# Layer 1's context prepared inside layer 0, first keys resized on VectorE, and a new order of one slot: a four-layer network on one Trainium2 core

## The chip, the cores and the metric

The kernel runs on one core of a Trainium2 chip, as one launch. The time is the device time of that core in microseconds (us). It was run three times: 6812.18 us is the median, 6793.82 and 6815.5 us are the ends. The core has TensorE (PE), VectorE (DVE), ScalarE (ACT), GpSimd (POOL) and SyncE (SP). Each takes its instructions in order; semaphores join them. SP here only issues DMAs.

## What is computed

An image `x` of shape (2, 128, 64, 64), all in float32, goes through four layers one after the other. Only what the change touches is written out:

```
layer 0:  x_norm = layernorm over channels, 4096 tokens per image
          for four orders (rows forward, rows reversed, columns forward, columns reversed):
              xh, z = x @ W_in ; xh = silu(causal conv of 4 taps (xh))
              dt, B, C = split(xh @ W_xp) ; dt = softplus(dt @ W_dt + b)
              h[t] = exp(dt*A) * h[t-1] + dt*B*xh        (256 channels x 16 states)
              y = sum over states of C*h + D*xh ; y = y * silu(z) ; y @ W_out
          x = x + fuse(the four outputs)
layer 1:  ctx = bilinear resize of context (4 images in, 2 used, each a mix over the batch axis;
                                            256 channels, 32x32 to 64x64)
          q = Wq x + bq ; k = Wk ctx + bk ; v = Wv ctx + bv
          x = x + gamma * conv3x3(softmax(q.k) v)
layer 2:  x = x + Wo softmax-attention(x) + bo
layer 3:  a second, smaller state-space layer on 16-channel groups, group norm, silu
```

The resize commutes with the 1x1 convolutions. So the kernel mixes the context images (weights 3/7, 3/7, 1/7), projects them to keys and values at 32x32, stores these four small images in DRAM (`low`), and resizes pieces of them when attention needs them.

## The kernel before

**Layer 0** works on 64 chunks of 512 tokens: 2 images x 2 orders x 2 directions x 8 chunks. I number them 0 to 63. A chunk has 16 units `u`, each a 128x1024 piece of the state. The loop `for k, c in enumerate(chunks)` holds a loop over 16 slots `s`, and the order of every engine's queue is the order in which this loop issues (`tc.manual_schedule()`). In slot `s` of chunk `c` it issues, in this order:

- POOL: `s_dbu(s+2)` (L330), the product that feeds a scan two slots later; three buffers `dbu`
- DVE: `s_scan(s)` (L374), the recurrence; then an optional step `V[s]`
- DVE or POOL: `s_hc(s-1)` (L386 on DVE, L384 on POOL for units 0, 5, 9, 11, 14), state times C
- ACT: `s_da(s+1)` (L343, two instructions, into one of two PSUM buffers), `s_fix(s+1)` (L355 and L358: the carry between chunks is added into `dbu`), `s_hst` (L379), then the steps `A[s]`
- PE: `y0` and the sums over states `s_y` (L390, L397), then the step `M[s]`, then `s_pc` (L363), which spreads C for a later `s_hc`

The steps `A`, `M`, `V` prepare the next chunks. The chunk after this one is `new`, the one after that `nxt`. For `nxt`: `px(0)` in `M[8]` and `px(1)` in `M[10]` (L228, the 4-tap convolution as four matmuls each), their results read by `x_(0)` in `A[9]` and `x_(1)` in `A[12]` (L237), `xsilu` in `A[13]`, and `pd` in `M[15]` (L267). For `new`: `xd_` in `A[0]` (L272, reads the result of `pd`, and issues two DMAs of `rows`), `pt(0)` in `M[0]` (L287, needs `xd_`), `abs_`, `e_exp`, `e_ln` in `A[1]` to `A[3]` (L294 to L300; `e_ln` costs two loads of an activation table). All of `px`, `pd`, `pt`, `pz`, `po` and the norm's matmuls share one PSUM bank, `misc`: each waits until the reader of the one before is done. The gate `yg_` (L404, DVE) reads the finished sums: `yg_(0)` in slot 10, `yg_(1)` in slot 1 of the next chunk.

Twelve chunks do a part of the layernorm as well: chunks 0 to 4 (`norms[0..3]` and its second halves) and 15 to 23. I call chunks 1 to 4 and 16 to 23 norm chunks, and the other chunks normal.

**Opening** of layer 0 (before chunk 0): both images of `x` are loaded (L74), the first four norm blocks are done, the first chunk's quantities are made.

**Between the layers**: when layer 0's buffers are free, SP loads `m3`, `cw3`, `dtw3`, `m1`, `m2` and four context images (L662 to L726); PE and DVE combine two weights of layer 2 (`wvo`, `bo`, L705 to L710); DVE mixes (L731 to L733); PE projects into four banks (L740), ACT copies with bias (L742) and pads by one row at each end (L744, L745); SP stores `low` (L746). Then `resize` makes the first two key pieces in five steps: load a piece `lo` (L799), `wide` on ACT (L804 to L807), `wide2` on POOL (L813), `high` on ACT (L818, L819), `high2` on POOL (L824). Then the first query, and then the attention of layer 1.

**Layers 1 and 2** run as one pipeline of 64 groups of 256 queries, 16 slots each; the later pieces of keys and values are put into slots by `piece` and `put`. **Layer 3** is not touched but for where `m3`, `cw3` and `dtw3` are loaded.

Of the kernel before, what the change touches and what calls it, by code (L numbers as in the profile page):

```python
# [56 lines left out]
def conv_seq_kernel(ctx: ExitStack, tc: tile.TileContext, a: dict, out: bass.AP):  # L57
# [12 lines left out]
    xin = a["x"].rearrange("b c h w -> c b (h w)")  # L70
    for b in range(B):
        for lo, hi in ((0, 1), (1, 2), (2, 4), (4, 8)):
            sl = slice(lo * T, hi * T)
            nc.sync.dma_start(x[:, b, sl], xin[:, b, sl])  # L74
    nc.scalar.dma_start(vec, a["vec"])
    nc.scalar.dma_start(cst, a["cst"])

    def v(name):
        return vec[:, _V[name] : _V[name] + 1]
# [8 lines left out]
    act(aneg, vec[:, _VA0:_NV], AF.Exp)  # L88
    nc.vector.tensor_scalar(aneg, aneg, -1.0, None, ALU.mult)

    with ExitStack() as c0:
# [21 lines left out]
        nc.scalar.dma_start(m0, a["m0"][:, 0 : 256 + 2 * ND])  # L116
        nc.scalar.dma_start(w_dt[64:ND, :], a["wdt"])
        w_xT, w_out, w_fT = mt[:, 0:256], mt[:, 256:512], mt[:, 512:1024]
        w_zT = m0[:, 0:256]
# [20 lines left out]
        for t in (xn, xnt):  # L140
            nc.vector.memset(t[:, 0:3], 0.0)
            nc.vector.memset(t[:, L + 3 : L + 6], 0.0)

        def gq(u):
# [298 lines left out]
        with tc.manual_schedule():  # L443
# [64 lines left out]
            for i in range(2):  # L508
                nc.vector.tensor_scalar(diag_d[:, i, :], ident, v(f"dp{i}"), None, ALU.mult)
            for j in (2, 3):  # L510
                act(sqs[j], xcs[j], AF.Square)
# [19 lines left out]
            act(r[:, 8:16], vr[:, 8:16], AF.Sqrt, bias=eps)  # L531
            nc.vector.reciprocal(r[:, 8:16], r[:, 8:16])
            for i in range(2):
                c1.px(i, ba[i])
# [21 lines left out]
            for k, c in enumerate(chunks):  # L556
# [15 lines left out]
                if new is not None:  # L572
                    A[0] = (new.xd_,)
                    M[0], A[1] = lambda: new.pt(0), (lambda: new.abs_(0),)
                    M[1], A[2] = lambda: new.pt(1), (lambda: new.abs_(1), new.e_exp)
                    A[3] = (new.e_ln,)
                    M[4], V[5] = lambda: new.pt(0), lambda: new.dt_(0)
                    M[5], V[6] = lambda: new.pt(1), lambda: new.dt_(1)
                    G[7], G[8] = lambda: new.dtu_(0), lambda: new.dtu_(1)
                    if not new.rev:  # L580
                        M[6], A[7] = lambda: new.pz(0), (lambda: new.z_(0),)
                        M[13], A[14] = lambda: new.pz(1), (lambda: new.z_(1),)
                if nxt is not None:
                    M[8], A[9] = lambda: nxt.px(0), (lambda: nxt.x_(0),)
                    M[10], A[12] = lambda: nxt.px(1), (lambda: nxt.x_(1),)
                    A[13] = (nxt.xsilu,)
                    M[15] = nxt.pd
                if lp is not None:
                    A[3] = (*A[3], lp.ln, lp.exp)
                    A[6] = (lp.rows,)  # L590
                    M[7], V[8] = lp.scale, lp.mul
                    A[10] = (lp.affine,)
                if ln is not None:
                    M[12], V[13] = ln.center, ln.sub
                    A[14] = (*A.get(14, ()), ln.square)
                    M[14], A[15] = ln.var, (ln.keep,)
                if k in turns:
                    A[11] = (lambda: turn(turns[k]),)

                for s in range(16):  # L600
# [9 lines left out]
                    if s in G:  # L610
                        G[s]()

                    if c1 is not None:
                        c1.s_da(u1)
                        c1.s_fix(u1)
# [4 lines left out]

                    if s in (3, 11):
                        c.y0(s // 11)
                    for cy, e in ((c, s), (old, s + 16)):
                        for u in pairs.get(e, ()) if cy is not None else ():
                            cy.s_y(u)
                            cy.s_y(u + 1)
                    if s in M:
# [33 lines left out]
    dtw3 = gt([P, 32], "dtw3", late)  # L661
    nc.sync.dma_start(m3, a["m3"])  # L662
    nc.sync.dma_start(cw3, a["cw3"].partition_broadcast(P))
    nc.sync.dma_start(dtw3, a["dtw3"].partition_broadcast(P))

# [3 lines left out]
    with ExitStack() as c1:  # L669
# [7 lines left out]
        ps = c1.enter_context(tc.tile_pool(name="ps1", bufs=1, space=PSUM))  # L677
        dr = c1.enter_context(tc.tile_pool(name="dr1", bufs=1, space=bass.MemoryType.DRAM))

        m1 = gt([P, 1792], "m1", wp)  # L680
        m2 = gt([P, 512], "m2", wp)
        nc.sync.dma_start(m1, a["m1"])
        nc.sync.dma_start(m2, a["m2"])
        w1qT = m1[:, 0:128]
        w1kT = m1[:, 128:384].rearrange("p (k c) -> p k c", k=2)
        w1vT = m1[:, 384:640].rearrange("p (k c) -> p k c", k=2)
        w1pT = m1[:, 640:1792].rearrange("p (k c) -> p k c", k=9)
# [11 lines left out]
        def small(tag, shape, bufs=None):  # L699
# [3 lines left out]
        wvo = gt([P, P], "wvo", wp)  # L703
        pw = misc()
        mm(pw[:, :P], lhsT=w2v, rhs=w2oT, start=True, stop=True)  # L705
        nc.vector.tensor_copy(wvo, pw[:, :P])
        bo = gt([P, 1], "bo", wp)
        pw = misc()
        mm(pw[:, :1], lhsT=w2oT, rhs=v("bv2"), start=True, stop=True)
        nc.vector.tensor_add(bo, v("bo2"), pw[:, :1])  # L710

# [4 lines left out]
        nc.gpsimd.memset(pad, 0.0)  # L716


        low = [[dr.tile([P, 34, 32], F32, tag=f"low{b}{w}", name=f"low{b}{w}") for w in range(2)]
               for b in range(B)]  # L720
        cfeat = a["ctx"].rearrange("b (k p) h w -> p b k (h w)", p=P)
        with ExitStack() as cc:
            cx = cc.enter_context(tc.tile_pool(name="ctx", bufs=1))
            feat = [cx.tile([P, 2, 1024], F32, tag=f"ct{j}", name=f"ct{j}") for j in range(4)]
            for j in range(4):
                nc.sync.dma_start(feat[j], cfeat[:, j])  # L726
            for b in range(B):

                wts = (3 / 7, 3 / 7, 1 / 7) if b == 0 else (1 / 7, 3 / 7, 3 / 7)
                mix = cx.tile([P, 2, 1024], F32, tag="mix", name="mix", bufs=2)  # L730
                nc.vector.tensor_scalar(mix, feat[b], wts[0], None, ALU.mult)  # L731
                nc.vector.scalar_tensor_tensor(mix, feat[b + 1], wts[1], mix, ALU.mult, ALU.add)
                nc.vector.scalar_tensor_tensor(mix, feat[b + 2], wts[2], mix, ALU.mult, ALU.add)  # L733

                for w, (wT, bias) in enumerate(((w1kT, v("bk1")), (w1vT, v("bv1")))):
                    t = cx.tile([P, 34, 32], F32, tag="lo", name="lo", bufs=2)
                    for hf in range(2):
                        pl = bank("s", bufs=4)
                        for k in range(2):
                            mm(pl, lhsT=wT[:, k, :], rhs=mix[:, k, hf * T : (hf + 1) * T],  # L740
                               start=(k == 0), stop=(k == 1))
                        act(t[:, 1 + 16 * hf : 17 + 16 * hf, :], pl.rearrange("p (h w) -> p h w", w=32),  # L742
                            AF.Identity, bias=bias)
                    nc.scalar.copy(t[:, 0:1, :], t[:, 1:2, :])  # L744
                    nc.scalar.copy(t[:, 33:34, :], t[:, 32:33, :])  # L745
                    nc.sync.dma_start(low[b][w], t)  # L746

        sp_ = c1.enter_context(tc.tile_pool(name="s", bufs=13))

        class Job:  # L750
# [42 lines left out]
            def resize(self, w, qd, dst):  # L793

                st = {}

                def load():
# [11 lines left out]
                def wide2():  # L809
                    hz = st["hz"] = small("hz", (P, 10, W), bufs=1)  # L810
                    o = hz.rearrange("p h (w two) -> p h w two", two=2)
                    for e in range(2):
                        nc.gpsimd.tensor_add(o[:, :, :, e], st["lo"], st["q"][:, :, 2 * e : 2 * e + 32])  # L813

# [6 lines left out]
                def high2():  # L821
                    o = dst.rearrange("p (h two w) -> p h two w", two=2, w=W)
                    for e in range(2):
                        nc.gpsimd.tensor_add(o[:, :, e, :], st["t"], st["hz"][:, 2 * e : 2 * e + 8, :])  # L824

# [101 lines left out]
        class Conv:  # L927
# [13 lines left out]
            def end(self):  # L941
# [3 lines left out]
                nc.gpsimd.tensor_add(xo, xo, t)  # L945

        jobs = [Job(1, 0), Job(1, 1), Job(2, 0), Job(2, 1)]
        groups = [Group(j, g) for j in jobs for g in range(NG)]
# [34 lines left out]
        with tc.manual_schedule():  # L983
            for qd in range(2):
                for f in jobs[0].key_piece(qd):
                    f()
            piece(1, jobs[0], "key_piece", 2)
            piece(5, jobs[0], "key_piece", 3)
            for qd in range(4):
                piece(10 + 5 * qd, jobs[0], "value_piece", qd)  # L990
            groups[0].q = jobs[0].query(0)

# [555 lines left out]
```

## Time and profile before

| what | value |
|---|---|
| three runs | 6793.82, 6812.18 (median), 6815.5 us |
| the profiled execution's own time | 6810.44 us |
| its span in the profile | 6808.7 us |
| busy: PE, DVE, ACT, POOL | 6005.6, 5524.3, 4461.8, 5362.4 us |
| granted TensorE clock, mean | 0.857 |

The span is 1.7 us shorter than the execution's own time, and that time is 1.7 us below the median. In the profile the first scan starts at 57.2 us, layer 0's last matmul ends at 3480.5 us, the first score of layer 1 starts at 3523.7 us, and layer 3 starts near 5690 us. A row of the timeline gives the start, the duration and in brackets the idle time before it with what ended that; rows of one kind that follow each other are merged (x2, x8).

### The profile page before, as it was taken

The numbers are of one execution on the slowest core, as the hardware profiler recorded it, in microseconds if no ns is written. First come the engines' busy times: TensorE is split into PE (matmuls) and PEld (weight loads), VectorE is DVE, ScalarE is ACT, GpSimd is POOL, SyncE is SP. The second block draws the span as 40 slices with busy tenths as digits, with TensorE's granted clock in tenths as the row PEclk, the third lists the DMA queues.
The fourth block names the chain that finished last, engine by engine and source line by source line (L and its number), as shares of the span: only waits on it lengthen the run. The fifth ranks groups of instructions, "written<-read, shape, count | busy, mean of one in ns | idle before, by whom it ended". The sixth has DMA issues, their size and how long they took to land. (4 is left out here: it accounts for less than half of the span.)

```text
span 6808.7 us, 67303 instructions
## 1 busy us (share of the span) xinstructions
PE 6005.6 (88%) x20652; PEld 2821.7 (41%) x20652; DVE 5524.3 (81%) x4499; ACT 4461.8 (66%) x7666; POOL 5362.4 (79%) x2487
## 2 busy tenths in 40 slices
PE   8888888888888888888879999999999997888888
PEld 2222222222222222222238887787788884222222
DVE  7999999999999999999966665565566675787777
ACT  7887778877788777887745664555456564434342
POOL 6899998899999999999956664555566666777776
PEclk7777777777778777777779999999999998988888
DMA  6565655566566656665630000000000001222221
GB/s 170 138 149 145 157 145 140 137 154 150 141 159 152 157 143 154 150 154 146 148 93 2 4 4 1 1 1 1 1 1 13 1 1 61 75 71 72 90 75 67
DMA packets 352652, 616.51 MB, mean 91 GB/s; under 512 B 72473, under 2 KB 74786, under 8 KB 351650
## 3 DMA queue, kind: packets, MB, share of 16 engines
q1 hardware_dynamic: 351552, 610.44, 35.2%
q8 instruction: 162, 2.65, 0.2%
q14 instruction: 200, 1.64, 0.1%
q10 hardware_dynamic: 738, 1.78, 0.1%
HBM read 496.45 MB, written 115.47 MB: 90 GB/s over the span
## 5 line engine op out<-in xcount | busy, mean ns | idle before, releaser
L330 POOL TENSOR_TENSOR dbu<-dus,bs 128x1024 f32<-128x1024 f32 x1024 | 2404.0, 2374 | 157.0 <-DVE h L374 141.1
L374 DVE TENSOR_TENSOR_SCAN h<-da,hst,dbu 128x1024 f32<-128x1024 f32 x896 | 2094.3, 2345 | 77.8 <-ACT dbu L358 75.0
L343 ACT ACTIVATE da<-dts,aneg 128x512 f32<-128x512 f32 (+1 forms) x2048 | 1412.6, 690 | 443.7 <-DVE h L374 404.1
L890 POOL TENSOR_TENSOR sum<-sum,sc 128x1024 f32<-128x1024 f32 x384 | 906.8, 2362 | 496.7 <-ACT sc L885 493.1
L852 ACT COPY sc<-s 128x512 f32<-128x512 f32 x1024 | 598.1, 585 | 867.7 <-PE s L847 753.5
L859 DVE TENSOR_TENSOR mx<-mx,s 128x512 f32<-128x512 f32 x896 | 610.1, 681 | 569.5 <-ACT sc L852 568.5
L847 PE MATMUL s<-q,k 128*128 128x256 f32 x4096 | 1058.0, 382 | 11.7 <-ACT q L833 8.4
L902 PE MATMUL av<-sc,v 128*128 128x256 f32 x4096 | 1049.6, 379 | 2.3 <-ACT sc L885 2.3
L397 PE MATMUL y<-hc,cst 128*32 128x512 f32 x4096 | 811.3, 760 | 179.2 <-DVE hc L386 103.8
L386 DVE TENSOR_TENSOR hc<-h,pc 128x1024 f32<-128x1024 f32 x704 | 844.9, 1200 | 0.1
L847 PEld LDWEIGHTS s<-q,k 128*128 128x128 f32 x4096 | 781.2, 192 | 146.2 <-issue 36.6
L902 PEld LDWEIGHTS av<-sc,v 128*128 128x128 f32 x4096 | 769.1, 190 | 103.1 <-ACT sc L885 3.7
L384 POOL TENSOR_TENSOR hc<-h,cs 128x1024 f32<-128x1024 f32 x320 | 758.2, 2369 | 1.3 <-issue 1.3
L363 PE MATMUL pc<-xd,sel 16*128 16x512 f32 x1024 | 713.4, 788 | 4.8 <-DVE hc L386 4.1
L1217 POOL TENSOR_TENSOR A<-A,D 128x1024 f32<-128x1024 f32 x224 | 525.9, 2365 | 225.2 <-DVE D L1222 200.3
L882 DVE TENSOR_TENSOR sc<-sc,pm 128x1024 f32<-128x1024 f32 x512 | 620.9, 1214 | 0.9 <-PE pm L878 0.9
L885 ACT ACTIVATE sc<-sc 128x1024 f32<-128x1024 f32 x512 | 542.3, 1059 | 8.6 <-DVE sc L882 8.1
L287 PE MATMUL misc<-xd,w_dt 9*128 9x512 f32 x504 | 386.5, 855 | 155.1 <-ACT x L426 83.6
L1210 ACT ACTIVATE A<-dtr,aneg 128x1024 f32<-128x1024 f32 (+1 forms) x256 | 246.0, 1032 | 380.8 <-PE y L1242 363.0
L397 PEld LDWEIGHTS y<-hc,cst 128*32 128x32 f32 x4096 | 104.9, 117 | 745.6 <-issue 337.4
L1228 DVE TENSOR_TENSOR A<-A,q 128x1024 f32<-128x1024 f32 (+1 forms) x256 | 276.9, 1082 | 148.4 <-PE q L1194 148.2
L1194 PE MATMUL q<-xs,lb 32*128 32x512 f32 x896 | 331.5, 712 | 72.0 <-DVE D L1204 65.7
(263 smaller groups left out, 8078.4 us busy)
## 6 DMA issues: line engine op xcount, KB each, us to landing
dts<-ddt SPq DMA_DIRECT2D x512, 256.0 KB, 5.5
dus<-ddu SPq DMA_DIRECT2D x512, 256.0 KB, 5.1
bs<-rows SPq DMA_DIRECT2D x1024, 64.0 KB, 4.9
cs<-rows SPq DMA_DIRECT2D x1024, 64.0 KB, 3.3
ddt<-dt SPq DMA_DIRECT2D x128, 256.0 KB, 2.0
ddu<-dtu SPq DMA_DIRECT2D x128, 256.0 KB, 4.1
dtr<-ddt SPq DMA_DIRECT2D x448, 64.0 KB, 1.9
rx<-ddx SPq DMA_DIRECT2D x448, 64.0 KB, 1.9
```

The costliest lines, as they stand in the source:

```text
L330: nc.gpsimd.tensor_mul(t, self.dus[q], _bc(self.bs[g], 1, [P, 2, T]))
L343: act(t[:, i, sl], self.dts[q][:, i, sl], AF.Exp, scale=an[:, g, 2 * q + i : 2 * q + i + 1])
L363: mm(t, lhsT=sel[32:48, 4 * g : 4 * g + 4, :].rearrange("p n d -> p (n d)"), rhs=self.xd[32:48, :], start=True, stop=True)
L374: nc.vector.tensor_tensor_scan(ho, ai, bi, init, ALU.mult, ALU.add)
L384: nc.gpsimd.tensor_mul(t, self.h[u], _bc(self.cs[gq(u)[0]], 1, [P, 2, T]))
L386: nc.vector.tensor_mul(t, self.h[u], _bc(self.pc[u // 2], 1, [P, 2, T]))
L397: mm(self.y[q // 2][r : r + 32, :], lhsT=sum4, rhs=self.hc[u][:, i, :], start=False, stop=(u % 8 >= 6), skip_group_check=True)
L847: mm(p[:, o, :], lhsT=j.k[m // 8][:, m % 8 * P : m % 8 * P + P], rhs=self.q, start=True, stop=True)
L859: nc.vector.tensor_max(self.mx, self.s[0][:, 0:2, :] if u == 1 else self.mx, self.p[u])
L882: nc.vector.tensor_sub(s, s, _bc(self.pm[:, :], 1, [P, 4, NQ]))
L890: nc.gpsimd.tensor_add(self.sum, self.s[0] if w == 1 else self.sum, self.s[w])
L902: mm(self.av, lhsT=self.job.v[m // 8][:, m % 8, :], rhs=self.s[u // 2][:, m % 4, :], start=(m == 0), stop=(m == 31))
```

## The change

It has four parts.

1. **The context.** Image 1 of `x` is no longer loaded in the opening; it is loaded in chunks 9 to 12, one quarter each. The four context images are loaded by SP in the opening instead, into the free halves of `xnt`, two `h` and two `dbu` buffers. VectorE mixes them in place: `mixed(0)` behind the two `diag_d` instructions, `mixed(1)` behind the second reciprocal. In chunks 0 to 7 a step `Low.conv` (two matmuls into `misc`) is `M[8]` and `Low.out` (one ACT instruction into a free part of `x`, two DMAs to `low`) is in `A[9]`.
2. **The order of layer 0.** In all chunks `px(0)` moves from `M[8]` to `M[9]`, `x_(0)` from `A[9]` to `A[10]` (behind `affine` in norm chunks). `xd_` moves from the end of slot 0's ACT work to its front, ahead of `s_da(1)`, `s_fix(1)` and `s_hst`. The sums `y0` and `s_y` are issued ahead of ACT's part; on PE's own queue nothing changes by that, since only ACT instructions stood between.
3. **Between the layers.** Loads, mixing, projection, copies and stores of `low` are gone from there. The first piece of keys is loaded first, then the 128 columns of `m1` that the query needs, the second piece, and the rest of `m1` and `m2`. The first query stands between the first and the second key piece. The third and fourth key pieces are put one slot earlier (0 and 4 in place of 1 and 5). `wvo` and `bo` are made in slot 6, the loads for layer 3 are issued in slot 7.
4. **The resize.** `wide2` and `high2` of the four key pieces of image 0 run on VectorE in place of GpSimd.

```diff
-    for b in range(B):
-        for lo, hi in ((0, 1), (1, 2), (2, 4), (4, 8)):
-            nc.sync.dma_start(x[:, b, sl], xin[:, b, sl])
+    for lo, hi in ((0, 1), (1, 2), (2, 4), (4, 8)):
+        nc.sync.dma_start(x[:, 0, sl], xin[:, 0, sl])
...
+        w_kv = x[:, 1, 0:512].rearrange("p (w k c) -> p w k c", w=2, k=2)
+        nc.scalar.dma_start(x[:, 1, 0:512], a["m1"][:, 128:640])
...
+        for k in range(2):
+            nc.sync.dma_start(mix[0][k], cfeat[:, 0, k])
+        for j in (1, 2):
+            for k in range(2):
+                feat[j, k] = wt("h" if j == 1 else "dbu", NH if j == 1 else NDBU, (P, 1024))
+                nc.sync.dma_start(feat[j, k], cfeat[:, j, k])
+        for k in range(2):
+            nc.sync.dma_start(mix[1][k], cfeat[:, 3, k])
+        def mixed(b):
+            w = (3 / 7, 3 / 7, 1 / 7) if b == 0 else (1 / 7, 3 / 7, 3 / 7)
+            for k in range(2):
+                m = mix[b][k]
+                nc.vector.tensor_scalar(m, m, w[0 if b == 0 else 2], None, ALU.mult)
+                for j in (1, 2):
+                    nc.vector.scalar_tensor_tensor(m, feat[j, k], w[j - b], m, ALU.mult, ALU.add)
+        class Low:
+            def conv(self):
+                self.p = misc()
+                for k in range(2):
+                    mm(self.p, lhsT=w_kv[:, self.w, k, :], rhs=mix[self.b][k][:, self.hf * T : self.hf * T + T],
+                       start=(k == 0), stop=(k == 1))
+            def out(self):
+                t = x[:, 1, T * (1 + self.hf) : T * (2 + self.hf)]
+                act(t, self.p, AF.Identity, bias=v("bv1" if self.w else "bk1"))
+                nc.sync.dma_start(o[:, 32 + T * self.hf : 32 + T * self.hf + T], t)
+                ... # and one row of padding
...
                 if new is not None:
-                    A[0] = (new.xd_,)
...
-                    M[8], A[9] = lambda: nxt.px(0), (lambda: nxt.x_(0),)
+                    M[9], A[10] = lambda: nxt.px(0), (lambda: nxt.x_(0),)
...
-                    A[10] = (lp.affine,)
+                    A[10] = (lp.affine, *A.get(10, ()))
...
+                if k < 8:
+                    lw = Low(k // 4, k % 4 // 2, k % 2)
+                    M[8], A[9] = lw.conv, (*A.get(9, ()), lw.out)
+                if 9 <= k < 13:
+                    sl = slice(2 * T * (k - 9), 2 * T * (k - 8))
+                    nc.sync.dma_start(x[:, 1, sl], xin[:, 1, sl])
...
+                    if s in (3, 11):
+                        c.y0(s // 11)
+                    for cy, e in ((c, s), (old, s + 16)):
+                        for u in pairs.get(e, ()) if cy is not None else ():
+                            cy.s_y(u)
+                            cy.s_y(u + 1)
+                    if s == 0 and new is not None:
+                        new.xd_()
                     if c1 is not None:
                         c1.s_da(u1)
                         c1.s_fix(u1)
...
-                    if s in (3, 11):
-                        c.y0(s // 11)
-                    for cy, e in ((c, s), (old, s + 16)):
-                        ...
+                eng = nc.vector if self.b == 0 and w == 0 else nc.gpsimd
-                        nc.gpsimd.tensor_add(o[:, :, :, e], st["lo"], st["q"][:, :, 2 * e : 2 * e + 32])
+                        eng.tensor_add(o[:, :, :, e], st["lo"], st["q"][:, :, 2 * e : 2 * e + 32])
...
-            for qd in range(2):
-                for f in jobs[0].key_piece(qd):
-                    f()
-            piece(1, jobs[0], "key_piece", 2)
-            piece(5, jobs[0], "key_piece", 3)
+            k0, k1 = (jobs[0].key_piece(qd) for qd in range(2))
+            k0[0]()
+            nc.sync.dma_start(m1[:, 0:128], a["m1"][:, 0:128])
+            k1[0]()
+            nc.sync.dma_start(m1[:, 128:], a["m1"][:, 128:])
+            nc.sync.dma_start(m2, a["m2"])
+            for f in k0[1:]:
+                f()
+            groups[0].q = jobs[0].query(0)
+            for f in k1[1:]:
+                f()
+            piece(0, jobs[0], "key_piece", 2)
+            piece(4, jobs[0], "key_piece", 3)
...
-            groups[0].q = jobs[0].query(0)
+            put(6, second, thirds)
```

## The prediction, made before the changed kernel was run

> **What bounds the kernel now.** I read the 40 slices of the page first. They divide the span into layer 0 (VectorE and GpSimd nearly full), a dip, and layers 1 and 2 (TensorE full).
>
> ```profile
> PEclk7777777777778777777779999999999998988888
> DVE  7999999999999999999966665565566675787777
> POOL 6899998899999999999956664555566666777776
> ```
>
> Then the windows by class of chunk. After the colon stand the length and each engine's busy time.
>
> ```profile
> core 0: us, PE busy (x) PEld busy (x) DVE busy (x) ACT busy (x) POOL busy (x), PEclk, DMA share, GB/s
> 914.00:1371.00 457.00, 388.61 (x1068) 114.76 (x1066) 417.59 (x265) 378.44 (x732) 411.59 (x186) 0.77 0.57 140
> 1371.00:3478.00 2107.00, 1787.91 (x4750) 482.93 (x4749) 2037.54 (x1241) 1676.28 (x3176) 2041.11 (x917) 0.77 0.61 149
> 3478.00:3524.00 46.00, 21.25 (x44) 9.26 (x43) 12.05 (x9) 12.84 (x30) 10.07 (x8) 0.76 0.49 183
> ```
>
> The 40 last chunks take 2107/40 = 52.7 us with VectorE and GpSimd busy for 97% each: a new order can win back at most 1.7 us of VectorE's idle time in each. The eight norm chunks of the first row take 57.1 us, of which VectorE idles (457 - 417.6)/8 = 4.9 us. The last row is the passage from layer 0 to layer 1: 46 us in which no engine is busy for half the time. It holds the sure gain, so I read its timeline; then the waits of VectorE in layer 0, and one normal and one norm chunk.
>
> ```profile
> DVE h L374 <- ACT dbu L358: 75.0, 129, 1.4
> DVE dt L404 <- PE y L397: 38.8, 36, 2.4
> ```
>
> **The passage.** In before the chain is: layer 0's last matmul ends 3480.5, context loads, VectorE's mixing from 3491.2, projection, store of `low`, load of a piece, resize, query, first score.
>
> ```profile
> 3491.22 1.23 DVE L731 TENSOR_SCALAR mix<-ct 128x2048 f32<-128x2048 f32 x1 [0.99 <-DMA ct<-in_ctx_dram]
> 3499.68 16.60 PE L740 MATMUL s<-mix,m 128*128 128x512 f32 x32 [9.64 <-DVE mix L733]
> 3509.72 0.34 SPq L799 DMA_DIRECT2D lo<-low  x1
> 3512.01 0.47 ACT L804 ACTIVATE q<-lo 128x320 f32<-128x320 f32 x1
> 3514.43 1.59 POOL L813 TENSOR_TENSOR hz<-lo,q 128x320 f32<-128x320 f32 x2 [30.10 <-ACT lo L807]
> 3517.59 2.49 POOL L824 TENSOR_TENSOR k<-h,hz 128x512 f32<-128x512 f32 x2 [1.57 <-ACT hz L819]
> ```
>
> After: the load of `lo` goes out at 3480.6 and lands 2.3 later (here 3509.72 to 3512.01), 3482.9. `wide` has 0.47 + 0.20 + 0.21 + 0.47 = 1.35 of ScalarE. `wide2` and `high2` on VectorE have no row. The nearest are its 128x512 adds, 0.69 us; from above, GpSimd's own 0.80 and 1.25. I take 0.45 for a 320-element half and 0.69 for a 512-element half, by length: 0.9 and 1.4. `high` is 0.63 + 0.74. Sum: 2.3 + 1.35 + 0.9 + 1.37 + 1.4 = 7.3, and 0.4 of semaphores, so the first score starts near 3480.6 + 7.7 = 3488.3 instead of 3523.7, 35.4 us sooner. The query (0.59 on PE, 0.46 on ScalarE) lies beside the resize. What the passage did besides, two small products and the loads for layer 3, goes to slots 6 and 7, where ScalarE's copies set the pace. In group 0 the scores waited for keys too (VectorE's `mx` starts 4.4 us after the first score), and pieces 2 and 3 come a slot sooner and on a faster engine: I give 3.6 us for it, between 0 and 7. On the other side ScalarE must resize the second piece before its first copy of scores; that can eat up to 3. **-39** (-33 to -43).
>
> **The opening.** `mixed(0)` and `mixed(1)` are 6 instructions of 1024 elements each, half of the 1.23 and 2.29 rows: 2 x (0.62 + 1.15 + 1.15) = 5.8 us each. VectorE waits 14.54 us for ScalarE from 23.6 on and 6.34 us from 39.9 on, so both fit if their loads have landed. Image 1's loads go, the same 2.1 MB of context and 0.26 MB of weights come; some are late behind the first scan's data. **+1.5** (0 to 5).
>
> **`Low` in chunks 0 to 7.** Each chunk gains two matmuls (1.8 us: four 128x512 passes to a pair, 3.5 when the clock is half), one 0.69 ScalarE instruction and two DMAs on SP. They take the `misc` bank between `scale` and `px(0)`. In normal chunks PE has 15% idle and ScalarE 20%: 0.3 each for four. In norm chunks 1 to 4 the bank is the chain (norm product, `px`, `center`, `var`, `pd`), and I add the matmul and half of its reader: 2 each. **+9** (3 to 13). Image 1's quarter loads in chunks 9 to 12 are four issues of 0.5 us on SP's queue: nothing.
>
> **`px(0)` one slot later.** GpSimd and VectorE see it only through `misc`. In normal chunks `x_(0)` has 0.9 us to spare before `px(1)`. In norm chunks VectorE's `yg_(0)` waits 2.45 us behind `px(0)` today; those leave, but `sub` in slot 13 then waits for `center` behind a later `px(1)`, and most returns. The clock decides more: the same eight passes take
>
> ```profile
> 1176.54 5.63 PE L228 MATMUL misc<-xnt,wk 128*128 128x512 f32 x8
> 1184.15 3.70 PE L228 MATMUL misc<-xnt,wk 128*128 128x512 f32 x8
> ```
>
> at slots 8 and 10 of one chunk. In slot 9 `px(0)` may run in either. I take 0; the low end is 12 x 0.9 = 11 less (0.9 of the 2.45 is kept), the high end has four of twelve cold, 4 x 1.9 = +8. [...] These rows alone don't show what ended the fast state. [...]
>
> **`xd_` ahead of `da(1)`.** This adds a wait: `xd_` reads `pd`, and behind it on ScalarE stand `da(1)`, `fix(1)` and `hst`, for which scan 1 waits, and `fix(1)` holds GpSimd's next `dbu` through scan 1. Chunk 43 (scan 0 at 2369.5):
>
> ```profile
> 2368.50 3.52 PE L267 MATMUL misc<-xs,m 128*73 128x512 f32 x4
> 2369.62 1.42 ACT L343 ACTIVATE da<-dts,aneg 128x511 f32<-128x511 f32 x2 [0.23 <-DVE h L374]
> 2372.05 0.68 ACT L272 ACTIVATE xd<-misc,vec 73x512 f32<-73x512 f32 x1 [0.24 <-PE misc L267]
> 2386.93 2.35 DVE L374 TENSOR_TENSOR_SCAN h<-da,hst,dbu 128x1024 f32<-128x1024 f32 x1 [1.03 <-ACT dbu L358]
> ```
>
> `pd` ends 2.5 us after scan 0 starts. With `xd_` first, scan 1 starts 0.68 + 1.42 + 0.39 + 0.4 of semaphores = 2.9 us after `pd`'s end, here 5.4 instead of 3.4. But scan 5 is late anyway, by ScalarE's two table loads behind `fix(4)`, which waits for GpSimd (row 2386.93); that absorbs delays as long as `pd` ends within about 1.15 us of scan 0. Over 50 normal chunks with a following chunk 34 end later, and the sum of the excess is 26.9 us. Against it: `yg_(1)` no longer waits in slot 1 (about 0.3 x 50 = 15), and `pd` may come sooner, since `px(0)` beside `px(1)` keeps PE fast; if all of them came within the 1.15, the sum would be -15. Between 26.9 - 15 = +12 and -15 I take **+3** (-16 to +20). In norm chunks `pd` ends 3.5 to 5.1 after scan 0:
>
> ```profile
> 1147.33 0.69 ACT L272 ACTIVATE xd<-misc,vec 73x512 f32<-73x512 f32 x1 [2.27 <-PE misc L267]
> 1150.25 0.69 DVE L404 TENSOR_TENSOR dt<-sz,y 128x512 f32<-128x512 f32 x1 [1.78 <-PE y L397]
> ```
>
> There scan 1 moves from 3.4 to 7.2, and the 1.78 of `yg_(1)` behind it vanish: scan 2 moves by +1.9 with PE at half clock, by -0.4 with PE fast. Part is absorbed at scan 5. 12 chunks, **+3** (-5 to +23).
>
> **Sum** against the profiled 6810.4: -39 + 1.5 + 9 + 0 + 3 + 3 = -22.5, that is 6788. The median of the runs is 1.7 above this execution; I keep 6788.
>
> **The rivals.**
> - **A, as summed**: 6772 to 6806, 17 to either side, two thirds of the 26 that half the terms' ranges make with their squares added. Chance 0.44.
> - **B, layer 0 gets shorter too.** The waits of `yg_` (38.8 of them on PE) and part of the 75.0 on `dbu` go, as `pd` comes sooner with a warm PE. For it: VectorE idles 4.9 us in a norm chunk and these waits are named. Against: GpSimd is as full as VectorE. 12 x 2 + 50 x 0.3 = 39 less, of which `Low` takes 9 and sub's wait 8: -39 - 22 = -61, about 6750. Chance 0.22.
> - **C, slower: the wait of `xd_` for `pd` is paid in every chunk.** If the slack at scan 5 isn't there (GpSimd's loop of `dbu`, `fix`, scan moves with it), a normal chunk pays about 0.8 us and a norm chunk 1.9: 51 x 0.8 + 12 x 1.9 = 64, with 10.5 from opening and `Low`, less 39: +35, 6845. It decides from (39 - 10.5)/63 = 0.45 us per chunk. Chance 0.20.
> - **D, the gain is eaten**, within 0.3%: half of C's price, or groups of layer 1 that had been waiting for PE anyway; about 6808. Chance 0.14.
>
> **How the numbers follow.** The bound is 0.3%, 20.4 us, about what a measurement of this kernel can tell from no change: faster means below 6791.7. A lies below it with 0.58 of its chance, B wholly: 0.44 x 0.58 + 0.22 = 0.48. Slower is C, 0.20 of chance, the rest 0.32. The range goes down past B to 6742 and up into C to 6832, so that about 0.07 and 0.13 are left out.
>
> **What would show it.** Right: the first score some 8 us after layer 0's last matmul instead of 43; the window of chunks 24 to 63 within 0.3 us of 52.7 each; no `yg_(1)` waits. Scan 1 waiting on `dbu` or `da` for 2 us or more in normal chunks, with GpSimd's `dbu` waiting behind it, shows C. Norm chunks below 56 us show B. Wrong in the passage: a first score later than 12 us. Chunks 1 to 4 tell `Low` apart from the order, which chunks 16 to 23 have alone.

## The result: the passage gained what was forecast, and layer 0 gave it back

The changed kernel takes 6824.7 us (median; 6813.8 to 6837.8) beside 6805.95 for the one before (22 runs of each). The ratio is 1.0026, with an interval of [1.0019, 1.0033]: slower by 0.26%, just inside the 0.3% that I had called no change, where I had forecast 6788 and a small gain. The profiled execution took 6824.68 us, its span is 6822.9, 14.2 longer than before.

I read the passage first, since the sure gain was there. The timeline of the changed kernel (start, duration, engine, line, idle time before it):

```profile
3525.01 1.90 PE L472 MATMUL misc<-dt,wof 128*128 128x512 f32 x4
3527.04 0.34 SPq L827 DMA_DIRECT2D lo<-low  x1
3529.44 0.47 ACT L832 ACTIVATE q<-lo 128x320 f32<-128x320 f32 x1 [1.47 <-DMA m<-in_m_dram]
3530.72 0.90 DVE L841 TENSOR_TENSOR hz<-lo,q 128x320 f32<-128x320 f32 x2 [3.62 <-DMA lo<-low]
3533.08 1.29 DVE L852 TENSOR_TENSOR k<-h,hz 128x512 f32<-128x512 f32 x2 [1.46 <-ACT hz L847]
3534.48 0.76 PE L875 MATMUL s<-q,k 128*128 128x256 f32 x1 [3.69 <-ACT q L832]
```

Layer 0's last matmul ends at 3525.01 + 1.90 = 3526.9, the first score starts at 3534.5: 7.6 us, against 43.1 before (3480.5 to 3523.7). The forecast was 7.7, and it held part by part: ScalarE starts on `lo` 2.4 us after its load was issued (2.3 in the sum), the two halves of `wide2` take 0.90 us on VectorE (0.9), those of `high2` 1.29 (1.4). But the end of layer 0 has moved from 3480.5 to 3526.9: layer 0 is 46.4 us longer. The windows of the changed kernel, by class of chunk (length, then each engine's busy time; the chunk boundaries are the first scans):

```profile
core 0: us, PE busy (x) PEld busy (x) DVE busy (x) ACT busy (x) POOL busy (x), PEclk, DMA share, GB/s
110.10:352.10 242.00, 204.70 (x555) 60.56 (x547) 210.02 (x131) 194.48 (x389) 210.47 (x94) 0.76 0.56 138
939.30:1400.00 460.70, 380.68 (x1070) 113.59 (x1062) 416.64 (x264) 377.46 (x731) 417.71 (x186) 0.77 0.56 139
1400.00:3520.70 2120.70, 1790.59 (x4739) 478.99 (x4740) 2036.00 (x1239) 1668.73 (x3176) 2074.69 (x917) 0.78 0.60 148
```

Chunks 1 to 4 take 60.5 us each (57.1 before), 16 to 23 take 57.6 (57.1), 24 to 63 take 53.0 (52.6). The last row holds the surprise. VectorE is as busy as before, ScalarE a little less, but GpSimd has 2074.7 us of work where it had 2041.1, with the same 917 instructions. The groups of the page say which. Before:

```profile
L330 POOL TENSOR_TENSOR dbu<-dus,bs 128x1024 f32<-128x1024 f32 x1024 | 2404.0, 2374 | 157.0 <-DVE h L374 141.1
```

and after:

```profile
L383 POOL TENSOR_TENSOR dbu<-dus,bs 128x1024 f32<-128x1024 f32 x1024 | 2463.8, 2444 | 149.6 <-DVE h L427 134.9
```

The column after the bar is the busy time and the mean of one instruction in ns. The same product of the same shape takes 2444 ns in place of 2374, 1024 times, on an engine that was 97% busy in chunks 24 to 63. No line of the diff changes it. And in the waits of VectorE in layer 0 the ones for `yg_` (38.8 us and more) are gone. The scans' wait for `dbu` has grown from 75.0 to 89.3 us, and two kinds are new (waiting instruction, what ended the wait, us in total, times, longest; `xc` is the step `sub`):

```profile
DVE h L427 <- ACT dbu L411: 89.3, 129, 1.5
DVE h L427 <- ACT hst L432: 43.3, 13, 4.6
DVE xc L214 <- PE misc L210: 17.7, 11, 2.0
```

The second line is above all scan 1 of the norm chunks, 26.3 us of it in seven waits in chunks 16 to 23: ScalarE stands at `xd_`, which waits for `pd`. A norm chunk (20), first ScalarE, then VectorE:

```profile
1174.89 0.68 ACT L325 ACTIVATE xd<-misc,vec 73x512 f32<-73x512 f32 x1 [4.52 <-PE misc L320]
1177.68 2.35 DVE L427 TENSOR_TENSOR_SCAN h<-da,hst,dbu 128x1024 f32<-128x1024 f32 x1 [4.05 <-ACT hst L432]
```

So there are three suspects for the 46.4 us: the slower product, the order, and `Low`. The theories that the runs were to tell apart:

- **P (places).** The changed kernel asks for its work buffers in another sequence (the context borrows `h` and `dbu` buffers first), so `dbu` and the others lie elsewhere in SBUF, and that alone slows GpSimd's product.
- **O (order).** The new order costs what chunks 16 to 63 show, and the slower product is only a sign of it.

### The profile page after: what moved, and what is told of

The parts are those of the page before. It is cut to its first block, busy times and chain, and to the rows that moved or that the text cites. A ratio compares the mean times of both kernels' runs of the same rounds, so it can differ in the third digit from the quotient of the medians.

```text
span 6822.9 us, 67295 instructions
## 1 busy us (share of the span) xinstructions
PE 6009.7 (88%) x20652; PEld 2817.3 (41%) x20652; DVE 5537.8 (81%) x4521; ACT 4446.9 (65%) x7658; POOL 5398.1 (79%) x2471
## 5 line engine op out<-in xcount | busy, mean ns | idle before, releaser
L383 POOL TENSOR_TENSOR dbu<-dus,bs 128x1024 f32<-128x1024 f32 x1024 | 2463.8, 2444 | 149.6 <-DVE h L427 134.9
L427 DVE TENSOR_TENSOR_SCAN h<-da,hst,dbu 128x1024 f32<-128x1024 f32 x896 | 2092.7, 2342 | 138.7 <-ACT dbu L411 89.3
L450 PE MATMUL y<-hc,cst 128*32 128x512 f32 x4096 | 894.6, 762 | 202.4 <-DVE hc L439 184.7
L439 DVE TENSOR_TENSOR hc<-h,pc 128x1024 f32<-128x1024 f32 x704 | 843.5, 1198 | 18.3 <-PE y L450 10.8
L875 PEld LDWEIGHTS s<-q,k 128*128 128x128 f32 x4096 | 780.3, 191 | 140.2 <-issue 29.3
L340 PE MATMUL misc<-xd,w_dt 9*128 9x512 f32 x504 | 361.4, 803 | 153.7 <-ACT x L479 71.7
L450 PEld LDWEIGHTS y<-hc,cst 128*32 128x32 f32 x4096 | 124.8, 120 | 864.4 <-DVE hc L439 428.4
```

What stands on the lines that cost most here:

```text
L383: nc.gpsimd.tensor_mul(t, self.dus[q], _bc(self.bs[g], 1, [P, 2, T]))
L427: nc.vector.tensor_tensor_scan(ho, ai, bi, init, ALU.mult, ALU.add)
L439: nc.vector.tensor_mul(t, self.h[u], _bc(self.pc[u // 2], 1, [P, 2, T]))
L450: mm(self.y[q // 2][r : r + 32, :], lhsT=sum4, rhs=self.hc[u][:, i, :], start=False, stop=(u % 8 >= 6), skip_group_check=True)
L875: mm(p[:, o, :], lhsT=j.k[m // 8][:, m % 8 * P : m % 8 * P + P], rhs=self.q, start=True, stop=True)
```

## Experiments

### The places, with nothing else changed

To the kernel before one request was added, which puts `dbu` right behind `hc`, as in the changed kernel:

```diff
+        early = wt("dbu", NDBU, (P, 1024))
+        nc.vector.memset(early[:, 0:1], 0.0)
```

> The kernel before with one line more: a buffer of dbu is asked for at the start, so that dbu, bs, dus, cs and the other work buffers lie in the same SBUF places as in the changed kernel; one tiny memset is added and nothing is moved in any queue. Theory P (places): GpSimd's product dbu takes 2374 ns before and 2444 ns in the changed kernel because its operands lie elsewhere; here it takes about 2440 too, and layer 0 gets longer by 20 to 45 us, so 6825 to 6850 where before is near 6806. Rival O (order): the places mean nothing, dbu stays at 2374 ns and the time is that of before within 5 us.

Measured: 6836.9 us, ratio 1.0046 [1.0034, 1.0058]. The product takes 2427 ns, layer 0's last scan ends 25.9 us later than before, and chunks 24 to 63 take 53.0 us each, exactly as in the changed kernel:

```profile
1379.60:3500.40 2120.80, 1779.60 (x4744) 480.41 (x4742) 2036.81 (x1239) 1676.12 (x3176) 2072.45 (x917) 0.77 0.60 148
```

The other way round: in the changed kernel thirteen buffers are requested in the old sequence before the context's.

```diff
+        for tag, n, shape in (("xc", 1, (P, T)), ("sq", 1, (P, T)), ("r16", 1, (P, 16)), ...
+                              ("dus", 2, (P, 4 * T)), ("cs", 4, (P, T))):
+            early = wt(tag, n, shape)
+            nc.vector.memset(early[:, 0:1], 0.0)
```

> The changed kernel with thirteen work buffers asked for in the old sequence before the context's buffers, so that dbu, dus, bs and cs lie where they did before; tiny memsets are added in the opening. Theory P: dbu takes 2374 ns again and layer 0 loses 20 to 40 us, some 6790 to 6805, faster than before. Rival O: dbu stays near 2444 ns and the time stays near 6825.

Measured: 6800.3 us, ratio 0.9989 [0.9981, 0.9998]; the product 2369 ns; layer 0 22.0 us shorter than in the changed kernel. Its chunks 1 to 4 and 24 to 63:

```profile
110.80:351.10 240.30, 202.38 (x551) 59.78 (x548) 210.02 (x132) 194.42 (x389) 207.00 (x94) 0.77 0.55 139
1398.10:3498.80 2100.70, 1790.05 (x4740) 476.07 (x4740) 2034.43 (x1239) 1666.05 (x3176) 2040.79 (x917) 0.79 0.61 149
```

Theory P is right for these 22 us, in both directions, and the sign of the whole change hangs on them. Chunks 24 to 63 take 52.5 us each here, so 20 of the 22 us stood there; chunks 1 to 4 stay at 60.1.

### The order, part by part

`xd_` alone moved in the kernel before:

```diff
-                    A[0] = (new.xd_,)
...
+                    if s == 0 and new is not None:
+                        new.xd_()
                     if c1 is not None:
                         c1.s_da(u1)
```

> The kernel before with xd_ alone moved ahead of da(1) and fix(1) in slot 0. Theory O in the form of rival C: 0.4 to 0.8 us per normal chunk and 1 to 2 per norm chunk, together +25 to +60 us. Theory P: the order costs little, within 10 us of before, with dbu at 2374 ns.

Measured: 6840.7 us, 1.0045 [1.0033, 1.0058], with the product at 2371 ns. Layer 0 is 28.0 us longer: 1.1 to 1.2 in each norm chunk, on average 0.3 to 0.4 in chunks 9 to 15 and 24 to 63, nothing in 5 to 8. Alone, the move is rival C at about half its price (28.0 where C has 64), and VectorE's waits say so: its scans wait 85.7 us for `hst`, a kind that the kernel before doesn't have.

Then `px(0)`. The text below speaks of both moves; the edit that ran under it moves `px(0)` and `x_(0)` alone, and its numbers are read as that:

```diff
-                    M[8], A[9] = lambda: nxt.px(0), (lambda: nxt.x_(0),)
+                    M[9], A[10] = lambda: nxt.px(0), (lambda: nxt.x_(0),)
...
-                    A[10] = (lp.affine,)
+                    A[10] = (lp.affine, *A.get(10, ()))
```

> The kernel before with the whole new order of layer 0 (xd_ first, px(0) in slot 9, x_(0) in slot 10), without the context's move. Theory O: layer 0 is longer by some 24 us (0.43 in each normal and 0.5 in each norm chunk, as chunks 16 to 63 of the changed kernel show), 6830. Theory P: as before or a few us less, 6795 to 6810.

Measured: 6826.1 us, 1.0032 [1.0020, 1.0044]. But the sum hides two opposite parts. Its windows, chunks 16 to 23 and 24 to 63:

```profile
918.30:1354.80 436.50, 375.16 (x1070) 107.61 (x1070) 416.16 (x264) 376.94 (x731) 410.32 (x185) 0.80 0.59 146
1354.80:3486.30 2131.50, 1802.32 (x4743) 483.26 (x4741) 2038.64 (x1239) 1671.65 (x3176) 2041.69 (x917) 0.76 0.60 147
```

Norm chunks fall to 436.5/8 = 54.6 us, 2.5 less each; normal chunks rise to 53.3, 0.7 more each. Both moves, the two edits above together, in the kernel before:

> The kernel before with both moves of layer 0's order, px(0) in slot 9 and xd_ ahead of da(1); the context stays between the layers and the work buffers stay in their places. px(0) alone gave +0.7 us per chunk in 24 to 63 and -2.5 per chunk in 16 to 23; xd_ alone gave +0.3 and +1.1. If the two simply add: 24 to 63 at 53.6 us each, 16 to 23 at 55.7, about +30 us in all, 6835. If they need each other (xd_ first makes use of the earlier end of pd that px(0) beside px(1) brings): 24 to 63 at 52.5 and 16 to 23 at 57.8, as in the changed kernel with the old places; the time within 8 us of before, 6800 to 6815.

Measured: 6814.6 us beside 6816.4, ratio 0.9998 [0.9989, 1.0006]. The parts do not add (28.0 alone and 11.8 alone at the end of layer 0, 9.8 together); the second reading was right:

```profile
921.00:1383.50 462.50, 383.48 (x1072) 114.00 (x1071) 416.62 (x264) 377.74 (x731) 410.46 (x185) 0.77 0.56 138
1383.50:3484.30 2100.80, 1790.06 (x4739) 476.11 (x4740) 2034.83 (x1239) 1665.98 (x3176) 2040.88 (x917) 0.79 0.61 149
```

Chunk 43 shows why. With `px(0)` moved alone (PE, then VectorE; scan 0 at 2367.4):

```profile
2364.90 1.94 PE L267 MATMUL misc<-xs,m 128*73 128x512 f32 x4
2370.35 2.07 PE L287 MATMUL misc<-xd,w_dt 9*128 9x512 f32 x2 [2.46 <-ACT xd L272]
2374.35 0.69 DVE L404 TENSOR_TENSOR dt<-sz,y 128x512 f32<-128x512 f32 x1 [1.26 <-PE y L397]
```

and with both (scan 0 at 2381.2):

```profile
2378.72 1.94 PE L267 MATMUL misc<-xs,m 128*73 128x512 f32 x4
2380.99 0.68 ACT L272 ACTIVATE xd<-misc,vec 73x512 f32<-73x512 f32 x1
2381.72 1.12 PE L287 MATMUL misc<-xd,w_dt 9*128 9x512 f32 x2
```

With `px(0)` beside `px(1)`, `pd` takes 1.94 us in place of 3.52 (the clock granted to it is 1.00 in place of 0.54) and ends 0.6 us before scan 0 in place of 2.5 after it. The chunk is no exception: of the 38 chunks 25 to 62 `pd` ends after scan 0 in 31 before, in 3 with `px(0)` moved alone and in 4 with both. `xd_` in its old place can't use that: it stands behind `da(1)` and `hst`, PE stands 2.46 us at `pt(0)`, the next two passes take 2.07 instead of 1.12 (granted clock 0.50 instead of 1.00), and the sums behind them hold `yg_(1)`, which waits 30.2 us for them in chunks 24 to 63 where it waited 10.8 before. With `xd_` first it runs at once. In the normal chunks the two moves need each other. In the norm chunks `pd` comes late whatever `px(0)` does (`var` is ahead of it in the bank): in 16 to 23 it ends 4.4 us after scan 0 on average before, 3.9 with `px(0)` moved alone and 4.5 with both. There `xd_` first is a loss of 57.8 - 54.6 = 3.2 us.

So the order was split by class of chunk, in the changed kernel with the old places:

```diff
-                    if s == 0 and new is not None:
+                    if s == 0 and new is not None and lp is None:
                         new.xd_()
...
+                    if lp is not None:
+                        A[0] = (new.xd_,)
```

> The changed kernel with the old places of the work buffers, and with xd_ ahead of da(1) only in the chunks that don't follow a chunk with a layernorm part; in chunks 1 to 4 and 16 to 23 it goes back behind slot 0's other ScalarE work. If the norm chunks lose because scan 1 waits there for pd through xd_ (3.5 us on hst), they fall to 54.6 us each for 16 to 23, as with px(0) alone, and by 2 to 3 us for 1 to 4: 30 to 38 us less than with the old places alone, 6762 to 6772. If their time is set by the misc bank and not by that wait, nothing changes: 6800.

Measured: 6761.7 us, ratio 0.9932 [0.9918, 0.9947], faster than both kernels. Chunks 16 to 23 take 438.1/8 = 54.8 us, 24 to 63 52.5:

```profile
925.90:1364.00 438.10, 376.34 (x1068) 108.18 (x1061) 416.24 (x263) 377.01 (x731) 410.49 (x185) 0.80 0.59 146
1364.00:3463.60 2099.60, 1779.71 (x4743) 475.45 (x4741) 2034.71 (x1239) 1667.97 (x3176) 2041.09 (x917) 0.79 0.61 149
```

VectorE's waits for `hst` are gone from chunks 16 to 23 (26.4 us with the old places alone), and in chunk 20 scan 1 starts without a wait, with `xd_` behind the work that feeds it:

```profile
1150.80 0.68 ACT L331 ACTIVATE xd<-misc,vec 73x512 f32<-73x512 f32 x1 [1.39 <-PE misc L326]
1150.49 2.34 DVE L433 TENSOR_TENSOR_SCAN h<-da,hst,dbu 128x1024 f32<-128x1024 f32 x1
```

### The price of `Low`

The eight `Low` steps were taken out of the changed kernel with the old places; the stored images are filled with a piece of `x`.

```diff
-                if k < 8:
-                    lw = Low(k // 4, k % 4 // 2, k % 2)
-                    M[8], A[9] = lw.conv, (*A.get(9, ()), lw.out)
+                if k < 4:
+                    nc.sync.dma_start(low[k // 2][k % 2].rearrange("p h w -> p (h w)"), x[:, 0, 0:1088])
```

> The changed kernel with the old places, without the eight small projections in chunks 0 to 7: the stored small images are filled with a piece of x, so the context's part of the output is left out. Theory: Low costs 2.5 us in each of chunks 1 to 4 and 1 us in each of chunks 0 and 5 to 7, 14 us; then chunks 1 to 4 take 57.8 as 16 to 23 do, and the time is some 6786. Rival: chunks 1 to 4 are long because of the order or because of the loads beside them, and then they stay at 60 and the time at 6800.

Measured: 6778.2 us, 0.9947 [0.9935, 0.9959]. Layer 0 ends 16.7 us sooner than with `Low` (14 expected): 2.1 in each of chunks 1 to 4 (60.1 to 58.0), 1.5 in each of 5 to 7, 2.2 in chunk 0. That is 14.8 in the chunks that have the step; the other 1.9 came in later chunks, where the two kernels have the same code. Chunks 1 to 4 now stand as 16 to 23 do (57.9):

```profile
108.50:340.60 232.10, 192.91 (x535) 57.42 (x532) 208.99 (x132) 191.91 (x385) 207.30 (x94) 0.76 0.59 146
```

### Which place

Seven more placements in the kernel before, one execution each, asked what about the place matters. The edits are requests like those above, for other buffers.

> The kernel before with dus, the first source of GpSimd's product, placed ahead of the other work buffers in place of dbu; dbu stays where it was, bs and dts move up by 16384 bytes. If it is dbu's own place that slows the product, it stays at 2374 ns; if the places of the sources or their distances count, it changes to 2400 ns or more.

> The kernel before with dbu placed between dtu and dus: dbu lies 24 KB of each partition lower than before, dus and cs 12 KB higher, bs and dts where they were. If dbu is slow only next to hc and the small buffers, it stays at 2374 ns here; if every place but the last is slow (or the places of dus and cs count), it takes 2400 ns or more.

> The kernel before with dbu placed right behind bs: bs where it was, all later buffers 12 KB higher. Between the slow place (2427 to 2444 ns, low) and the old one (2374 ns, high) this is a third distance from hc: 2374 ns if only the neighbourhood of hc is slow, 2420 ns or more if it is the low half of the work buffers or the new places of dus, dts and cs.

> The kernel before with dbu placed behind xc and sq, 4 KB of each partition higher than in the slow placement; all other work buffers but xc, sq and r16 lie as in the slow one. If the slow product needs dbu right behind hc, it takes 2374 ns here; if the low neighbourhood or the places of the other buffers make it slow, 2420 ns or more.

> The kernel before with e and cs placed first: bs, xs, xd lie exactly as in the slow placement, dbu lies where it was before. If dbu's own place makes the product slow, it takes 2374 ns here; if the place of bs does, 2420 ns or more.

> The kernel before with dbu 12 KB of each partition higher than in the slow placement, behind xc, sq and xs; bs, dts, dus and cs lie exactly as in the slow placement. dbu was slow at 12 KB and 16 KB lower and took 2374 ns from 12 KB higher on: this run halves the gap. Either outcome is open; 2374 ns here would also clear bs, dts, dus and cs of it.

> The kernel before with dbu placed ahead of h and hc, so below them; bs, dts, dus and cs lie as in the slow placement. If a place near hc is what makes dbu slow, 2374 ns or a smaller excess; if the low end of the work buffers is slow, 2420 ns or more again.

In the table the first four rows are medians and the last seven single executions, beside which the kernel before took 6813 to 6816 us.

| kernel | first byte of `dbu` in a partition | its remainder by 128 | mean of the product, ns | time, us |
|---|---|---|---|---|
| before | 208032 | 32 | 2374 | 6805.95 |
| changed | 130144 | 96 | 2444 | 6824.7 |
| `dbu` early | 130144 | 96 | 2427 | 6836.9 |
| old places | 208032 | 32 | 2369 | 6800.3 |
| `dus` early | 208032 | 32 | 2373 | 6804.6 |
| `dbu` before `dus` | 183456 | 32 | 2373 | 6815.0 |
| `dbu` behind `bs` | 154784 | 32 | 2374 | 6798.1 |
| `bs` as in the changed | 208032 | 32 | 2374 | 6799.8 |
| `dbu` behind `sq` | 134240 | 96 | 2442 | 6826.0 |
| `dbu` behind `xs` | 142496 | 32 | 2373 | 6813.8 |
| `dbu` lowest | 101472 | 96 | 2440 | 6845.8 |

My guesses on the neighbours fell one by one. Two readings sort all these rows. One is the height: the product is slow up to 134240 and fast from 142496 on. The other is the remainder: `r16` is a buffer of 64 bytes, and what is requested ahead of it lies 64 bytes off from what comes behind it. (In the row "`dus` early" it is `dus` that leaves 96, and the product stays fast.) The last run told them apart on the changed kernel itself, with `r16` requested first, so that `dbu` moves by 64 bytes, to 130208, between two slow places:

```diff
+        early = wt("r16", 1, (P, 16))
+        nc.vector.memset(early[:, 0:1], 0.0)
```

> The changed kernel with one tile of 64 bytes, r16, asked for ahead of the context's buffers: dbu moves up by 64 bytes, as do xc and sq; everything else stays. In all placements so far dbu was slow where its place divided by 128 leaves 96 (130144, 134240, 101472) and fast where it leaves 32 (142496, 154784, 183456, 208032), as dus and bs leave 32. If that remainder decides, dbu takes 2374 ns here and the time is that of the old places, 6790 to 6810 and 0.3 to 0.45% below the changed kernel's. If the distance to the buffers below it decides, it stays at 2430 ns or more and at 6820 to 6835.

```profile
L385 POOL TENSOR_TENSOR dbu<-dus,bs 128x1024 f32<-128x1024 f32 x1024 | 2403.5, 2372 | 179.3 <-DVE h L429 163.3
```

Measured: 2372 ns, 6814.1 us, ratio 0.9992 [0.9983, 1.0001], where the changed kernel has 1.0026 (the median lies above the 6790 to 6810 that I expected; the kernel before took 6814.75 beside it); layer 0's last scan ends 22.8 us sooner than in the changed kernel. The height is out, and the 64 bytes are the cause of the slower product. (`xc` and `sq` move by them too, but they leave 96 in the kernel before as well, with the fast product.)

Three things stay open. The number 128 is a choice: remainders by 256 or 512 sort the rows as well. Why the 64 bytes count is not shown: GpSimd's other product, of `h` and `cs`, always writes `hc` at remainder 96 and takes 2363 to 2370 ns where `dbu` is fast, so it isn't the remainder of the output alone; where `dbu` is slow, that product is slower too (2372 to 2410 ns), though in three of the four slow kernels its output hasn't moved. And the mean of the product doesn't set the loss by itself: layer 0's last scan ends 14.8 us later than before with `dbu` behind `sq` (2442 ns) and 33.2 later with `dbu` lowest (2440 ns).

### The resize on VectorE

The kernel with `xd_` by class, with all resizes on GpSimd (a single execution, then five) and once more as it was:

```diff
-                eng = nc.vector if self.b == 0 and w == 0 else nc.gpsimd
+                eng = nc.gpsimd
```

> The kernel of the run with xd_ by class, with the resize of all key pieces on GpSimd as it was before. From the rows of the kernel before (0.80 and 1.25 us for a half on GpSimd, against 0.45 and 0.65 on VectorE) the first score of layer 1 comes 2 x 0.35 + 2 x 0.60 = 1.9 us later after layer 0's last matmul: 9.5 in place of 7.6 us; and if group 0 waits for keys, groups 0 and 1 take 3 us more in sum; if it waits for ScalarE, they take the same.

> The run with xd_ by class and all resizes on GpSimd, timed against the same with the first keys on VectorE. By the passage alone VectorE is 1.9 us faster; by the one look at groups 0 and 1 (64.9 us on GpSimd, 67.2 on VectorE) GpSimd is 2.3 faster there: the two medians within 3 us of each other, which these runs can't tell apart; more than 6 us either way would be a cost or a gain of the resize that the passage doesn't show.

> The same kernel as in the run with xd_ by class, once more beside the run with all resizes on GpSimd: 0.992 to 0.995 of the time before, as then.

Measured on GpSimd: 6764.0 us in the single execution, then 6764.1 us, 0.9931 [0.9919, 0.9943]. As it was: 6770.6, 0.9935 [0.9918, 0.9952]. From layer 0's end to the first score it is 9.4 us on GpSimd and 7.5 on VectorE; groups 0 and 1 then take 64.9 and 67.3. Sums: 74.3 and 74.8. The first score came later by 2.0 us, 1.9 expected; the groups did not take 3 us more, as they would if they waited for keys. In the whole time these runs tell no difference; the fourth part of the change brings nothing that can be measured. The first two groups of kernels whose code there is that of before took from 63.1 to 67.9 us, so the second pair of numbers proves little by itself.

## Why the prediction was wrong

The time lies in the stated range, between D's 6808 and C's 6845, but neither tells its cause. The sign was wrong: a gain was forecast and a loss came. By the steps of the sum, with what the traces measure:

| step | forecast, us | measured, us | from |
|---|---|---|---|
| passage to the first score | -35.4 | -35.6 | 43.13 to 7.57 |
| group 0 | -3.6 | -0.2 | groups 0 and 1: 67.75 to 67.55 |
| opening | +1.5 | +0.4 | first scan 57.15 to 57.55 |
| `Low` | +9 | +16.7 | run without it |
| order, both moves | 0 + 3 + 3 = +6 | +9.8 | both in the kernel before |
| places | not seen | +22.0 | changed kernel against old places |
| sum | -22.5 | +13.1 | |

The spans differ by +14.2, so the sum is near, but in part by luck: the four terms of layer 0 come from different pairs of kernels and add to 48.9, where its end moved by 46.4, and from the first score to the end the changed kernel took 3.4 us more (3288.4 against 3285.0), less than kernels with the same code there differ by (3274 to 3292 us with the code of before, 3277 to 3302 with that of the changed kernel).

- **The missing term is the failed step.** For the context's loads into free buffers of `h` and `dbu` I counted time and traffic alone. The step that requests `dbu` so early also fixed where it lies. I had listed instructions, queues and buffers, and for none of them did I ask whether the durations that I took from the trace of before would hold. The sum left GpSimd's product at its old duration of 2374 ns, and it took 2444. Without the 22.0 us the kernel would have been where "old places" is, 0.9989: no change, still not the gain of the forecast.
- **`Low` was mis-sized.** I took 0.3 us for a normal chunk and 2 for a norm chunk. The norm chunks were right (2.1). Chunk 0 paid 2.2 and chunks 5 to 7 1.5 each. That PE's idle share did not cover it because the two matmuls and their reader stand in the one bank ahead of `px(0)` fits, but no run shows it.
- **Group 0 was mis-sized.** I gave 3.6 us for keys that come sooner, and 0.2 came. On GpSimd, with the keys later, the first two groups took no longer either (64.9 against 67.3), so no run shows them waiting for keys.
- **The opening stayed in its range by luck.** I counted 2.1 MB of context. Its eight loads are of 512 KB each, 4.2 MB, and the first scan starts 0.4 us later all the same.
- **The order came out near its sum, from parts that I had wrong.** That the sum was near is luck. With `px(0)` moved alone the norm chunks win 2.5 us each, where I kept 0.9 at best and took nothing: in chunks 16 to 23 VectorE's waits in front of `yg_` fall from 29.3 to 9.0 us, and only 7.7 return in front of `sub`. The price of `xd_` first in a norm chunk is 3.2 us, not 1.9 or -0.4: it eats that gain, which I had no way to see from a sum of separate terms. In normal chunks the case in which PE stays fast held: `pd` at 1.94 us ends before scan 0, and 24 to 63 take 52.5 each with both moves.
- **The clock.** I left open how fast `px(0)` would run in slot 9. With the move alone its eight passes take 3.70 us in norm chunk 20, at a granted clock of 1.00, where they took 5.63 at 0.65, and in the normal chunk above `pd` is fast. The slower passes came in the kernel that moves `px(0)` and leaves `xd_`: two of `pt(0)` take 2.07 us at 0.50, behind 2.46 us of idle PE. That the idle time lowered the clock was not shown: no run varied it by itself.
- **The rivals.** C's mechanism is real when `xd_` moves alone (+28.0 at the end of layer 0, where I had 64 for its waits), and in the norm chunks of the changed kernel (43.3 us on `hst` in all of layer 0); in its chunks 24 to 63 it isn't there (1.0 us). B's shorter norm chunks came with `px(0)` alone and with `xd_` by class (54.6 and 54.8 us), not in the changed kernel (57.6).

## What to carry to other kernels

When a change requests a buffer at another time, its place and that of later buffers move, and every duration taken from the trace of before is open (here a product that no line touched went from 2374 to 2444 ns): compare the mean ns of the untouched groups first, and test it by requesting the buffers in the old sequence with nothing else changed. Cost two moves that share a chain together, not one by one: here each alone was slower and both together were neutral. And a move that pays in one class of an unrolled loop can lose in another; where the order is written out by hand, it can differ by class, and that split is what took this kernel, with the buffers in their old places, from a ratio of 0.9989 to 0.9932.

## What the runs showed of the hardware

A 128x1024 float32 product on GpSimd took 2367 to 2374 ns with its output buffer at a place that leaves 32 by 128, and 2427 to 2444 ns at 96, over ten different places or orders of the buffers. With the slow places, layer 0 of a kernel that keeps GpSimd 97% busy in chunks 24 to 63 got 22 to 26 us longer in the three pairs that were timed over several executions, and 15 and 33 in two single ones. In the last of the three pairs 64 bytes of place were the whole difference: 22.8 us at the end of layer 0 and 0.34% of the kernel's time.

Two passes of a matmul of 9 rows and 512 columns took 1.12 us at a granted clock of 1.00 and 2.07 at 0.50, the latter behind 2.46 us of idle PE; that the idle time was the cause was not shown.
